# A recurrence's division by logarithm, exponential and one Newton step on a Trainium2 core

## The chip, the core and the metric

The kernel runs on one core of a Trainium2 chip, in one launch. The metric is the device time of that core in microseconds (us). Before the change it was 1567.87 us, the median of three runs (1567.68 to 1570.94).

A core has five engines, each with its own queue of instructions: TensorE (PE in the profile, with PEld for its weight loads), VectorE (DVE), ScalarE (ACT), GpSimd (POOL) and SyncE (SP). [...] ScalarE evaluates functions such as exponential, sigmoid or square root from a table, and the profile shows an instruction ACT_TABLE_LOAD where the table is changed.

## The reference

A block of three kinds of layers, on x of 4 sequences of 1024 tokens with 256 channels, all in float32:

```python
x = x + attn_a(layernorm(x))     # time mixing with a recurrence (changed)
x = x + ffn(layernorm(x))        # mixture of 64 experts, 4 per token, and 2 shared
x = x + attn_b(layernorm(x))     # retention with 16 heads
x = x + ffn(layernorm(x))
```

The changed part is the recurrence of attn_a. For each channel, w is -exp(time_decay) and u is time_first; p, q and o are carried from token to token:

```python
no = maximum(o, u + kt)
A, Bc = exp(o - no), exp(u + kt - no)
y = (A * p + Bc * vt) / (A * q + Bc)
no2 = maximum(w + o, kt)
A2, B2 = exp(w + o - no2), exp(kt - no2)
p, q, o = A2 * p + B2 * vt, A2 * q + B2, no2
...
out = (sigmoid(r) * y) @ W_out.T     # r, v, k are projections of the normed x
```

## The kernel before

The 4096 tokens are cut into 8 segments of 512 tokens, two to a sequence. The residual x stays on the chip in 8 tiles. The program has four stages, and the change lies in the first:

1. attn_a, and of the first ffn the choice of experts, the sending of the token rows to pages in memory, and the shared experts (`stage_1`).
2. The first ffn's routed experts: pages are loaded with their expert's weights, computed, and gathered back.
3. attn_b (`stage_2`), interleaved with the end of stage 2 and the beginning of the second ffn.
4. The second ffn's routed experts and the stores.

In stage 1 every segment passes five steps that `wkv(i)` returns. `norm` (layernorm at L188 and transposes at L212) gives the normed rows with channels on the partitions. `inputs(hf)`, for each of two halves hf of 128 channels, projects k, v and r into three banks (TensorE, L641) and moves them out on ScalarE: k and v as copies (L652, L653), r as a sigmoid (L654). `weights(hf)` finds o for all 512 tokens by one scan along the tokens (L673), subtracts (L677), and makes a2, b2 and c by a Relu and an Exp each on ScalarE (L679 to L688). `sums(hf)` scans q and p (L697, L701), forms the denominator den = c + q (L706), its reciprocal (L707), the numerator c v + p (L708, L709), the product with r (L710) and y (L711), all on VectorE with tiles of 128 partitions by 512 elements. `output(h)` projects y (TensorE, L719) and adds it to x (L724). The tile den is b2's, the tile num is a2's; tags such as a2 and b2 have two buffers each.

In exact terms c is exp(min(u + k - o, CAP)): the Relu of L683 and the bias `cap` of L688 hold the exponent below CAP, which is 60.

After `output`, `Ffn.route(i)` chooses experts for the segment: norm, logits, pick, rank, place, weigh (mostly VectorE, L266 to L396; the softmax's Exp on ScalarE is at L392), then 16 indirect sends on GpSimd (L402). `Ffn.shared(i)` computes the shared experts: TensorE L426 and L439, Silu on ScalarE at L431, VectorE L432 and L444.

The order of the work has two sources. The list `tracks` at the end of `stage_1` gives each step a time in half segments, and `merge` calls the steps in the order of these times, so that the recurrence of later segments is written between the routing and the shared experts of earlier ones; the shared experts of the last segments are put off (`behind`). From that order the framework's scheduler makes each engine's queue, and it may let an instruction that is ready sooner go ahead. Semaphores and table loads are put in by the compiler, not by the code.

The routed stage loads pages that hold rows of all segments (`sent`), so its first load of rows (`rx`, L489) waits for the last segment's sends; the transposes at L501 wait for that load.

Of the kernel before, what the change touches and what calls it, by code (L numbers as in the profile page):

```python
# [14 lines left out]
AF = mybir.ActivationFunctionType  # L15
ALU = mybir.AluOpType
# [8 lines left out]
SEG = 512  # L25
# [8 lines left out]
GR = 32  # L34
NG = P // GR
CH = 128
CAP = 60.0
QS = 256


# [20 lines left out]
def hybrid_kernel(ctx: ExitStack, tc: tile.TileContext, a: dict, out: bass.AP):  # L61
    nc = tc.nc
# [21 lines left out]
    def bank(tag, name, shape=None):  # L84

        return psum.tile(shape or [P, SEG], F32, tag=tag, bufs=dict(A=4, B=3, C=1)[tag], name=name)
# [15 lines left out]
        out=upper, in_=ones, compare_op=ALU.is_ge, fill=0.0, base=-1,  # L102
# [85 lines left out]
    def layernorm(pool, tiles, i, rows=None):  # L188

        n = len(tiles)  # L190
        mv = pool.tile([P, n, 2], F32, tag="ln_mv", name=f"mv_{i}")
        for t, xt in enumerate(tiles):
            st = pool.tile([P, 6], F32, tag="ln_st", name=f"st_{i}_{t}")
            nc.vector.bn_stats(out=st, in_=xt)
            nc.vector.bn_aggr(out=mv[:, t, :], in_=st)
        rstd = pool.tile([P, n], F32, tag="ln_rstd", name=f"rstd_{i}")
        nc.scalar.activation(out=rstd, in_=mv[:, :, 1], func=AF.Sqrt, bias=eps_t)
        nc.vector.reciprocal(out=rstd, in_=rstd)
        off = pool.tile([P, n], F32, tag="ln_off", name=f"off_{i}")
        nc.vector.scalar_tensor_tensor(  # L200
            out=off, in0=mv[:, :, 0], scalar=-1.0, in1=rstd, op0=ALU.mult, op1=ALU.mult
        )
        where, bufs = rows or (pool, 2)
        xn = where.tile([P, n, D], F32, tag="ln_xn", bufs=bufs, name=f"xn_{i}")
        for t, xt in enumerate(tiles):
            nc.scalar.activation(
                out=xn[:, t, :], in_=xt, func=AF.Identity, scale=rstd[:, t : t + 1],
                bias=off[:, t : t + 1],
            )
        return xn  # L210

    def transposed(xn, n, xnT, i):  # L212

        for k in range(KC):
            tp = bank("B", f"tp_{i}_{k}", [P, n * P])
            for t in range(n):
                nc.tensor.transpose(
                    tp[:, t * P : (t + 1) * P], xn[:, t, k * P : (k + 1) * P], ident
                )
            nc.any.tensor_copy(out=xnT[:, k, :], in_=tp)  # L220
# [371 lines left out]
    def stage_1(ctx: ExitStack, ffn, pf):  # L592
# [21 lines left out]
        if MOST < NPAIR:  # L614
# [5 lines left out]
        nc.vector.tensor_scalar(  # L620
            out=u_cap, in0=u_t, scalar1=-1.0, scalar2=CAP, op0=ALU.mult, op1=ALU.add
        )
        nc.vector.memset(cap, CAP)

        carry = {}

        def wkv(i):


            st = {}  # L630

            def norm():
                xn = layernorm(pf, [xs[i][:, t, :] for t in range(TT)], f"a{i}")
                st["xnT"] = pa.tile([P, KC, SEG], F32, tag="xnTa", bufs=2, name=f"xnT_a{i}")
                transposed(xn, TT, st["xnT"], f"a{i}")

            def project(hf, what):
                ps = bank("A", f"rvk_{i}_{hf}_{what}")
                lo = what * D + hf * P
                for k in range(KC):  # L640
                    nc.tensor.matmul(  # L641
                        ps, lhsT=rvk[:, k, lo : lo + P], rhs=st["xnT"][:, k, :],
                        start=(k == 0), stop=(k == KC - 1),
                    )
                return ps

            def work(tag, hf, width=SEG, bufs=2):
                return pa.tile([P, width], F32, tag=tag, bufs=bufs, name=f"{tag}_{i}_{hf}")

            def inputs(hf):  # L650
                r, v, k = work("r", hf, bufs=3), work("v", hf, bufs=3), work("k", hf)
                nc.scalar.copy(out=k, in_=project(hf, 2))  # L652
                nc.scalar.copy(out=v, in_=project(hf, 1))  # L653
                nc.scalar.activation(out=r, in_=project(hf, 0), func=AF.Sigmoid)  # L654
                st[hf] = dict(r=r, v=v, k=k)

            def start(t, hf, n, first):
                if i % SPB == 0:
                    nc.vector.memset(t[:, 0:1], first)
                else:  # L660
                    nc.vector.tensor_copy(out=t[:, 0:1], in_=carry[hf][n][:, SEG:])
                carry.setdefault(hf, {})[n] = t

            def weights(hf):

                s = st[hf]
                k = s["k"]  # L670
                o = work("o", hf, SEG + 1, bufs=3)
                start(o, hf, "o", -1e38)
                nc.vector.tensor_tensor_scan(  # L673
                    out=o[:, 1:], data0=w_t[:, hf : hf + 1].to_broadcast([P, SEG]), data1=k,
                    initial=o[:, 0:1], op0=ALU.add, op1=ALU.max,
                )
                nc.vector.tensor_sub(out=k, in0=k, in1=o[:, :SEG])  # L677
                a2, b2, c = (work(n, hf) for n in ("a2", "b2", "c"))
                nc.scalar.activation(out=a2, in_=k, func=AF.Relu, bias=w_neg[:, hf : hf + 1])  # L679
                nc.scalar.activation(  # L680
                    out=b2, in_=k, func=AF.Relu, scale=-1.0, bias=w_t[:, hf : hf + 1]
                )
                nc.scalar.activation(  # L683
                    out=c, in_=k, func=AF.Relu, scale=-1.0, bias=u_cap[:, hf : hf + 1]
                )
                nc.scalar.activation(out=a2, in_=a2, func=AF.Exp, scale=-1.0)
                nc.scalar.activation(out=b2, in_=b2, func=AF.Exp, scale=-1.0)
                nc.scalar.activation(out=c, in_=c, func=AF.Exp, scale=-1.0, bias=cap)  # L688
                s.update(a2=a2, b2=b2, c=c)

            def sums(hf):
                s = st[hf]
                v, a2, b2, c = (s[n] for n in ("v", "a2", "b2", "c"))
                p, q = (work(n, hf, SEG + 1, bufs=3) for n in "pq")
                start(q, hf, "q", 0.0)
                start(p, hf, "p", 0.0)
                nc.vector.tensor_tensor_scan(  # L697
                    out=q[:, 1:], data0=a2, data1=b2, initial=q[:, 0:1], op0=ALU.mult, op1=ALU.add
                )
                nc.vector.tensor_mul(out=b2, in0=b2, in1=v)  # L700
                nc.vector.tensor_tensor_scan(  # L701
                    out=p[:, 1:], data0=a2, data1=b2, initial=p[:, 0:1], op0=ALU.mult, op1=ALU.add
                )
                y = pa.tile([P, SEG], F32, tag=f"y{hf}", bufs=2, name=f"y_{i}_{hf}")
                num, den = a2, b2
                nc.vector.tensor_add(out=den, in0=c, in1=q[:, :SEG])  # L706
                nc.vector.reciprocal(out=den, in_=den)  # L707
                nc.vector.tensor_mul(out=num, in0=c, in1=v)  # L708
                nc.vector.tensor_add(out=num, in0=num, in1=p[:, :SEG])  # L709
                nc.vector.tensor_mul(out=num, in0=num, in1=s["r"])  # L710
                nc.vector.tensor_mul(out=y, in0=num, in1=den)  # L711
                st[f"y{hf}"] = y

            def output(h):
                op = bank("B", f"op_{i}_{h}", [P, 2, D])
                for t in range(2):
                    c0 = (2 * h + t) * P
                    for hf in range(KC):
                        nc.tensor.matmul(  # L719
                            op[:, t, :], lhsT=st[f"y{hf}"][:, c0 : c0 + P], rhs=wout[:, hf, :],  # L720
                            start=(hf == 0), stop=(hf == KC - 1),
                        )
                xt = xs[i][:, 2 * h : 2 * h + 2, :]
                nc.vector.tensor_add(out=xt, in0=op, in1=xt)  # L724

            return norm, inputs, weights, sums, output


# [7 lines left out]
        while n < CH:  # L736
            nc.vector.tensor_scalar_mul(
                out=pw16[:, Z + n + 1 : Z + 2 * n + 1], in0=pw16[:, Z + 1 : Z + n + 1],
# [350 lines left out]
    with ExitStack() as held:  # L1089
# [19 lines left out]
        with right("turned") as pt:  # L1109
# [7 lines left out]
            for i in range(NSEG - SPB):  # L1117
                b, s = divmod(i, SPB)
# [98 lines left out]
```

## Time and profile before

| what | us |
|---|---|
| median of three runs | 1567.87 |
| the profiled execution | 1570.8 |
| its span (first to last instruction) | 1569.1 |
| PE busy | 1301.6 (83%) |
| DVE busy | 1019.6 (65%) |
| ACT busy | 706.5 (45%) |
| POOL busy | 515.2 (33%) |
| the last send of stage 1 starts | 418.61 |
| first TensorE work of the routed stage | 423.77 |

The profile is one execution. A row of a group gives the line of the code, the engine, the operation, output and input tiles with their shapes, the count, then the busy time and the mean duration of one in nanoseconds, then how long the engine was idle just before and what ended the idleness. A row in order of time gives start, duration, engine, line, operation and, in brackets, the idle time before it. Operations on one engine overlap a little, so the distance from one start to the next is less than the mean duration. Tiles' names leave out their buffer numbers: a2 and num are `a`, b2 and den are `b`.

The shares over the whole span are means over stages with different limits. Stage 1 takes the first 424 us, some 27% of the span.

### The profile page before, as it was taken

To read this page: it belongs to the slowest core of one execution; us is meant where nothing else is said; L and a number is where in the kernel's file an instruction comes from. 1 tells how busy PE (TensorE), PEld (TensorE's weight loads), DVE (VectorE), ACT (ScalarE), POOL (GpSimd) and SP (SyncE) were. 2 spreads that over 40 slices of the span, in tenths; PEclk is the share of its full clock that TensorE was granted. 3 is DMA by queue.
4 is the path that set the end of the run, shared out by engine and by line. 5 is a ranking of instruction groups with operands and counts; after the bars stand their busy time and mean duration, and the time that the engine had idled before them with its cause. 6 is when DMAs were issued, how large, how long until landed. Compare 5 with 4: busy or idle time off the path is not lost. (4 is left out here: it accounts for less than half of the span.)

```text
span 1569.1 us, 24370 instructions
## 1 busy us (share of the span) xinstructions
PE 1301.6 (83%) x8264; PEld 921.8 (59%) x8264; DVE 1019.6 (65%) x2447; ACT 706.5 (45%) x1364; POOL 515.2 (33%) x528
## 2 busy tenths in 40 slices
PE   4598999979588879999989699989996399999810
PEld 2254555646476756777765475667654388877710
DVE  5989899998355546666756693557647155566643
ACT  6586777743134453457433343344252144444410
POOL 0005244346300051323236543032034300155576
PEclk8699999999799999999979799999999699999955
DMA  9976921113499994666322211011012599999944
GB/s 354 394 226 116 289 71 47 41 47 114 161 302 329 330 324 129 201 197 201 117 90 81 81 55 54 0 55 38 18 54 82 177 330 322 319 352 366 357 139 127
DMA packets 192953, 278.13 MB, mean 177 GB/s; under 512 B 53683, under 2 KB 119094, under 8 KB 192822
## 3 DMA queue, kind: packets, MB, share of 16 engines
q1 hardware_dynamic: 144630, 166.34, 33.3%
q0 software_dynamic: 24576, 67.14, 13.2%
q10 hardware_dynamic: 23616, 43.00, 7.2%
q8 instruction: 70, 1.15, 0.3%
q14 instruction: 61, 0.50, 0.1%
HBM read 164.74 MB, written 124.26 MB: 184 GB/s over the span
## 5 line engine op out<-in xcount | busy, mean ns | idle before, releaser
L402 POOL DMA_INDIRECT sent<-xn_f,to_f x256 | 267.5, 1045 | 512.8 <-ACT w_f L392 285.7
L562 POOL DMA_INDIRECT gy_f<-made,to_f x256 | 245.0, 957 | 532.3 <-DMA rw_f<-wx 139.6
L513 PE MATMUL rg_f<-rxT_f,rw_f 128*128 128x128 f32 x1312 | 187.2, 286 | 15.1 <-DVE rxT_f L505 7.0
L513 PEld LDWEIGHTS rg_f<-rxT_f,rw_f 128*128 128x128 f32 x1312 | 166.2, 198 | 25.9 <-DVE rxT_f L505 17.1
L505 DVE COPY rxT_f<-rt_f 128x512 f32<-128x512 f32 x164 | 113.0, 689 | 102.1 <-PE rt_f L501 100.8
L573 DVE SCALAR_TENSOR_TENSOR x<-gy_f,w_f,x 128x256 f32<-128x256 f32 x256 | 121.5, 482 | 63.0 <-DMA gy_f<-made,to_f 59.4
L501 PE MATMUL rt_f<-ident,rx_f 128*128 128x128 f32 x656 | 108.3, 290 | 62.1 <-DMA rx_f<-sent 55.3
L532 PE MATMUL rp_f<-rw_f,rh_f 64*128 64x128 f32 x1312 | 135.7, 304 | 11.1 <-DVE rh_f L521 9.6
L518 ACT ACTIVATE rs_f<-rg_f 64x256 f32<-64x256 f32 x164 | 61.7, 376 | 174.1 <-PE rg_f L513 144.4
L426 PE MATMUL g_f<-xnT_f,f_swg 128*128 128x512 f32 x256 | 126.7, 610 | 2.1 <-DVE pm L983 1.5
L439 PE MATMUL o_f<-f_swd,sh_f 128*128 128x256 f32 x512 | 122.6, 387 | 5.5 <-DVE sh_f L432 3.1
L501 PEld LDWEIGHTS rt_f<-ident,rx_f 128*128 128x128 f32 x656 | 75.3, 146 | 86.0 <-DMA rx_f<-sent 49.8
L426 PE MATMUL u_f<-xnT_f,f_swu 128*128 128x512 f32 x256 | 123.3, 599 | 2.1 <-ACT k L652 1.5
L532 PEld LDWEIGHTS rp_f<-rw_f,rh_f 64*128 64x128 f32 x1312 | 101.8, 192 | 37.9 <-issue 12.2
L538 ACT COPY ry_f<-rp_f 128x256 f32<-128x256 f32 x248 | 87.6, 374 | 79.6 <-PE rp_f L532 47.0
L521 DVE TENSOR_TENSOR rh_f<-rg_f,rs_f 64x256 f32<-64x256 f32 x164 | 69.8, 426 | 71.1 <-ACT rs_f L518 68.3
L439 PEld LDWEIGHTS o_f<-f_swd,sh_f 128*128 128x128 f32 x512 | 95.7, 192 | 27.0 <-DVE sh_f L432 5.1
L983 DVE TENSOR_TENSOR pm<-sc,decay 128x512 f32<-128x512 f32 x128 | 84.0, 684 | 21.4 <-PE sc L975 13.8
L641 PE MATMUL rvk<-xnT_a,rvk 128*128 128x512 f32 x192 | 92.2, 621 | 1.0 <-DVE xnT_a L220 0.6
L431 ACT ACTIVATE sh_f<-g_f 128x512 f32<-128x512 f32 x64 | 38.0, 597 | 112.3 <-PE g_f L426 87.5
L522 ACT COPY rh_f<-rh_f 64x256 f32<-64x256 f32 x164 | 66.1, 403 | 38.8 <-DVE rh_f L521 34.5
L426 PEld LDWEIGHTS u_f<-xnT_f,f_swu 128*128 128x128 f32 x256 | 47.8, 191 | 57.5 <-issue 52.1
(227 smaller groups left out, 2252.6 us busy)
## 6 DMA issues: line engine op xcount, KB each, us to landing
rw_f<-wx SPq DMA_DIRECT2D x328, 192.0 KB, 4.4
rx_f<-sent SPq DMA_DIRECT2D x164, 256.0 KB, 4.9
made<-ry_f ACTq DMA_DIRECT2D x164, 256.0 KB, 4.6
sent<-zeros SPq DMA_DIRECT2D x7, 2048.0 KB, 15.6
sent<-zeros SPq DMA_DIRECT2D x1, 10240.0 KB
x<-in_x_dram SPq DMA_DIRECT2D x8, 512.0 KB
wx<-in_wg_dram SPq DMA_DIRECT2D x2, 2048.0 KB, 40.4
sent<-xn_f,to_f POOLq DMA_INDIRECT x256, 2.5
```

The lines of the kernel that those rows point to most:

```text
L402: ins = nc.gpsimd.indirect_dma_start(out=rows_sent[: pairs_until(i) * 2 * P, :], out_offset=bass.IndirectOffsetOnAxis(ap=st["to"][:, c : c ...
L426: nc.tensor.matmul(ps, lhsT=w[:, k, s], rhs=self.xnT[i][:, k, :], start=(k == 0), stop=(k == KC - 1),)
L439: nc.tensor.matmul(o[:, t, :], lhsT=st["h"][:, c, s], rhs=self.weights[2][:, c, :], start=(c == 0), stop=(c == NS - 1),)
L501: nc.tensor.transpose(tp[:, k, j, :], s["x"][:, j, k * P : (k + 1) * P], ident)
L505: nc.vector.tensor_copy(out=xT, in_=tp)
L513: nc.tensor.matmul(gu[:, j, :], lhsT=s["w"][:, j, k * 2 * F : (k + 1) * 2 * F], rhs=s["xT"][:, k, j, :], start=(k == 0), stop=(k == KC - 1),)
L532: nc.tensor.matmul(yp[:, j, :], lhsT=s["h"][r, j, :], rhs=s["w"][r, j, WD:], start=True, stop=True,)
L538: copy(out=y[:, :, c * P : (c + 1) * P], in_=yp)
L562: nc.gpsimd.indirect_dma_start(out=y[:, k, :], out_offset=None, in_=rows_made[: ready[t] * 2 * P, :], in_offset=bass.IndirectOffsetOnAxis( ...
L573: tc.keep_in_program_order(nc.vector.scalar_tensor_tensor(out=xs[i][:, t, :], in0=got[t][:, k, :], scalar=s["w"][:, c : c + 1], in1=xs[i][ ...
L641: nc.tensor.matmul(ps, lhsT=rvk[:, k, lo : lo + P], rhs=st["xnT"][:, k, :], start=(k == 0), stop=(k == KC - 1),)
L983: nc.vector.tensor_mul(out=pm, in0=ch[j]["sc"][g], in1=decay.rearrange("p (k g b) n -> p g k b n", k=KC, b=2)[:, g],)
```

## The change

The reciprocal of den is no longer one VectorE instruction. ScalarE computes exp(-ln(den)) into a new tile inv, in two instructions, and VectorE refines it by one Newton step: inv (den inv - 2) is the negative of the improved reciprocal, and the last product is multiplied by -0.5. The sigmoid is replaced by tanh: sigmoid(r) = 0.5 (1 + tanh(r / 2)), of which tanh(r / 2) is computed where the sigmoid was, the "1 +" is part of the product with the numerator, and the 0.5 is in the last product. den is formed right after the scan of q, ahead of the product and scan for p, and has a tile of its own. CAP goes from 60 to 40.

```diff
-CAP = 60.0
+CAP = 40.0
...
-                nc.scalar.activation(out=r, in_=project(hf, 0), func=AF.Sigmoid)
+                nc.scalar.activation(out=r, in_=project(hf, 0), func=AF.Tanh, scale=0.5)
...
+                den, inv = work("den", hf), work("inv", hf)
+                nc.vector.tensor_add(out=den, in0=c, in1=q[:, :SEG])
+                nc.scalar.activation(out=inv, in_=den, func=AF.Ln)
+                nc.scalar.activation(out=inv, in_=inv, func=AF.Exp, scale=-1.0)
                 nc.vector.tensor_mul(out=b2, in0=b2, in1=v)
                 nc.vector.tensor_tensor_scan(
                     out=p[:, 1:], data0=a2, data1=b2, initial=p[:, 0:1], op0=ALU.mult, op1=ALU.add
                 )
                 y = pa.tile([P, SEG], F32, tag=f"y{hf}", bufs=2, name=f"y_{i}_{hf}")
-                num, den = a2, b2
-                nc.vector.tensor_add(out=den, in0=c, in1=q[:, :SEG])
-                nc.vector.reciprocal(out=den, in_=den)
+                num = a2
                 nc.vector.tensor_mul(out=num, in0=c, in1=v)
                 nc.vector.tensor_add(out=num, in0=num, in1=p[:, :SEG])
-                nc.vector.tensor_mul(out=num, in0=num, in1=s["r"])
-                nc.vector.tensor_mul(out=y, in0=num, in1=den)
+                nc.vector.scalar_tensor_tensor(
+                    out=num, in0=s["r"], scalar=1.0, in1=num, op0=ALU.add, op1=ALU.mult
+                )
+                nc.vector.tensor_mul(out=den, in0=den, in1=inv)
+                nc.vector.scalar_tensor_tensor(
+                    out=inv, in0=den, scalar=2.0, in1=inv, op0=ALU.subtract, op1=ALU.mult
+                )
+                nc.vector.scalar_tensor_tensor(
+                    out=y, in0=num, scalar=-0.5, in1=inv, op0=ALU.mult, op1=ALU.mult
+                )
```

## The prediction

> **What bounds the kernel now.** I read the page's forty slices first, to find where the changed lines run (the first ten slices, some 400 us), then the busy time of each engine by stage, then the groups of that stage, then the engines' instructions in order of time. The chain of work that ended last can't be used here: it reaches back to 793 us only.
>
> Busy tenths by slice, from the page; a slice is 39 us:
>
> ```profile
> PE   4598999979588879999989699989996399999810
> DVE  5989899998355546666756693557647155566643
> ACT  6586777743134453457433343344252144444410
> ```
>
> In slices 2 to 10 the digits of DVE are 8 or 9 almost throughout, later only 3 to 7. So VectorE matters in this stage and not elsewhere. The first stage cut into stretches (start and end, length, then busy us of each engine with its instructions, granted TensorE clock, DMA share, GB/s):
>
> ```profile
> 0.00:80.00 80.00, 40.51 (x97) 19.98 (x98) 59.25 (x120) 47.04 (x71) 1.48 (x11) 0.79 1.00 374
> 80.00:220.70 140.70, 130.00 (x531) 77.54 (x529) 123.20 (x313) 102.61 (x147) 44.44 (x40) 0.98 0.71 183
> 220.70:264.26 43.56, 40.54 (x166) 23.74 (x165) 42.74 (x102) 33.30 (x48) 17.68 (x16) 1.00 0.13 47
> 264.26:320.00 55.74, 51.98 (x209) 30.34 (x208) 53.13 (x114) 45.32 (x64) 27.34 (x25) 1.00 0.16 59
> 320.00:378.90 58.90, 50.60 (x232) 32.04 (x232) 57.75 (x148) 22.29 (x35) 28.72 (x30) 0.97 0.25 76
> ```
>
> The third row is one segment, from the q scan of its first half to that of the next segment. DVE is busy 42.74 of 43.56 us (98%), PE 40.54 (93%, at full clock), ACT 33.30 (76%). VectorE ends last, but TensorE is only 2.2 us behind it. In the last row DVE works 57.75 of 58.90 us while PE has 8 us free.
>
> How the stage hands over, from the order of time: the last segment's VectorE chain ends in the row numbers, GpSimd sends from 397.86 to 419.6, and TensorE waits for those sends:
>
> ```profile
> 423.77 1.97 PE L501 MATMUL rt_f<-ident,rx_f 128*128 128x128 f32 x8 [16.64 <-DMA rx_f<-sent]
> ```
>
> All page loads of the routed stage wait for the last send, so time gained on the last segment's chain arrives at the end of the kernel nearly whole.
>
> **The change part by part.** The groups concerned, of 0 to 440 us (count, then busy us and mean ns of one, then idle time before):
>
> ```profile
> L707 DVE RECIPROCAL b<-b 128x512 f32<-128x512 f32 x16 | 53.5, 3345 | 0.0
> L654 ACT ACT_TABLE_LOAD x16 | 20.5, 1283 | 0.3
> L710 DVE TENSOR_TENSOR a<-a,r 128x512 f32<-128x512 f32 x16 | 10.8, 677 | 0.0
> L711 DVE TENSOR_TENSOR y<-a,b 128x512 f32<-128x512 f32 x16 | 10.8, 673 | 0.0
> L686 ACT ACTIVATE a<-a 128x512 f32<-128x512 f32 x16 | 10.0, 628 | 0.2
> L330 DVE SCALAR_TENSOR_TENSOR far_f<-rk_f,jump_f 128x256 f32<-128x256 f32 x8 | 3.3, 412 | 0.1
> L334 DVE TENSOR_TENSOR far_f<-far_f,end_f 128x256 f32<-128x256 f32 x7 | 2.9, 420 | 0.0
> ```
>
> *VectorE.* Sixteen reciprocals go (8 segments, 2 halves). Two multiplications become three-operand forms in place, and two operations are new: den times inv, and the Newton form. The rows L330 and L334 show that the three-operand form costs what the plain one does at equal shape (412 against 420 ns), so L710 and L711 keep their 0.68 us. The other end: L573's three-operand rows of that shape take 482 ns, with a scalar from a tile; 15% more on three instructions would be 0.3 us a half, 5 us in all. I take the equal price, as all scalars here are constants like L330's. Operations overlap in issue: a reciprocal starts at 353.33 and its successor at 356.59, a plain multiplication holds its place for 0.60 us (30.22 to 30.82). Net a half: -3.26 + 2 x 0.60 = -2.06 us; times 16 = -33 us of VectorE. A segment's 42.74 becomes 38.6.
>
> *ScalarE, the operations.* Logarithm and exponential on 128x512, priced by L686: 0.63 us, or 0.52 when back to back (a start at 117.06 us, the next at 117.58): about 1.2 a half, 19 us in all. Tanh takes Sigmoid's place at one price (597 ns row).
>
> *ScalarE, the table loads.* Here the price is least certain. L654 has a load before each of 16 Sigmoids; every change between Exp, Sqrt, Silu and Sigmoid shows one. [...] But in this trace each load stands at the activation that needs it, with no sign that a later one was looked at; a set chosen for the logarithm alone costs a second load at the exponential. So 1 to 2 loads a pair; I take 2: 32. Net 18 loads.
>
> What is a load worth? From ScalarE's order of time:
>
> ```profile
> 102.31 0.59 ACT L653 COPY v<-rvk 128x512 f32<-128x512 f32 x1 [0.62 <-PE rvk L641]
> 102.91 1.28 ACT L654 ACT_TABLE_LOAD   x1
> 104.21 0.60 ACT L654 ACTIVATE r<-rvk 128x512 f32<-128x512 f32 x1
> ```
>
> The copy ends at 102.90, the load runs from 102.91, Sigmoid from 104.21: 1.30 us in all. [...] By the row it is 18 x 1.3 + 19 = 42 us, 5.3 a segment: ScalarE at 38.6. [...] From both sides: 19 us (one load a pair, all of Sigmoid's gone) to 61 us (two a pair, none gone), ScalarE at 35.7 to 40.9.
>
> *The new wait.* On VectorE, den times inv waits for the exponential: 1.3 + 0.6 + 1.3 + 0.6 = 3.8 us from den with both loads. Between them stand the b2 product, the p scan, c times v, the addition of p and the product with r, some 3.6 us, so an idle ScalarE just meets it. If it is busy, everything queued behind on VectorE waits: the other half's scans, the layernorm statistics (and with them TensorE's transposes), the routing; the output product (L719) waits for y. The last half's chain still gets shorter: from q's end it was 8.1 us (0.6 + 1.2 + 3 x 0.6 + 3.27 + 2 x 0.6), now 0.6 + 3.8 + 3 x 0.6 = 6.2.
>
> *At nothing:* the cap is a constant in instructions that exist; den and inv are tiles of their own, so the b2 tile comes free earlier and nothing waits more. No DMA and no queue instruction moves.
>
> *The sum by stretch.* A segment now has PE 40.5, DVE 38.6, ACT 38.6 instead of 40.5, 42.7, 33.3. The binding engine is packed to 98% now; TensorE at 98% would give 41.3, a gain of 2.2. With three engines within 2 us of each other I don't expect that packing: ScalarE was busy 18.9 of 20 us between 220 and 240 us, just where the pair goes, and idle later. I take 0.5 us a segment, over 5.5 segments (80 to 320 us): 3 us. Between 0 and 80 us four reciprocals end, 8.2 us freed. PE waits there for xn_a, whose statistics follow the reciprocals of 30.82 and 58.17 in VectorE's order; ScalarE, four fifths busy from 20 to 60 us, gives part back: 3 us. From 320 to 379 us two reciprocals (335.87 and 353.33) sit on a VectorE without idle time, and ScalarE is only 38% busy: of 4.1 us freed I count 3.5. Sum: -9.5 us. Against the profiled execution (span 1569.1, with 1.7 us around it 1570.8 us) that is 1561.3; it lay 2.9 us above the median of the runs, 1567.87, so the forecast is 1558.
>
> **The rivals.** *TensorE bounds cleanly*: the pair always finds ScalarE free, the period falls to 41.3: 5.5 x 2.2 = 12, with 6 at the start and 4 at the end -22: 1546. For it: VectorE's waits on ScalarE are few today (11.9 us before q in the whole stage). Against: three close engines. *No difference*: PE's 40.5 plus its waits for xn_a already make 43.5, and only 0 to 3 us arrive: 1566. Against it: PE idles 8 us where VectorE has none. *Slower, ScalarE becomes the bound*: place, the half of each segment in which ScalarE runs exponentials, Silu and Sigmoid without a gap; price, up to 7.6 us a segment if Tanh saves no load and each pair takes two; it decides once ScalarE's busy time and its waits pass 43.5 us, from 40.9 busy on if it packs worse than 94%. ScalarE's order then holds up k, xn_a and Silu for TensorE, and VectorE waits at den times inv. At 45 us a segment: 5.5 x 1.5 = 8, the start and end gains gone: 1576. For it: its idle time now is mostly one wait of 8 us for the projection, which may not be usable. *It doesn't do what it says*: Tanh loads as Sigmoid did; that is contained in the bound above.
>
> **How the numbers follow.** A measurement can tell about 0.2% here, 3.1 us. Likeliest (1551 to 1564): 0.37; TensorE bound (1541 to 1551): 0.22; no difference (1565 to 1571): 0.14; slower (1571 to 1590): 0.27. So faster 0.59, same 0.14, slower 0.27. The range, 1543 to 1579, leaves out the far ends of the second and the last case; the likeliest case's own is 1551 to 1564.
>
> **What would show it.** No reciprocal of 128x512; two more VectorE rows of 0.68 us; VectorE's first 400 us 33 us lighter. Loads at Tanh nearly gone, loads at the logarithm and behind it 16 each; if the second set is missing, ScalarE is 20 us lighter than I say. The segment's period, 43.56 now, should be near 43; below 42 speaks for TensorE, above 44 for ScalarE, and then VectorE's waits name the exponential of inv. GpSimd's last send should start near 388 instead of 397.86. The later stages should keep their lengths; if they don't, the forecast is wrong for a reason that I have not seen.

## The result, and the profile after

| | before | after |
|---|---|---|
| median of six runs each | 1568.9 (1567.6 to 1576.58) | 1554.87 (1548.35 to 1561.01) |
| the profiled execution, its span | 1570.8, 1569.1 | 1561.01, 1558.9 |
| first TensorE work of the routed stage (the handover) | 423.77 | 411.87 |
| from there to the end | 1145.3 | 1147.0 |
| DVE busy | 1019.6 | 995.3 |
| ACT busy | 706.5 | 739.3 |

The kernel is faster: ratio 0.9917, 95% interval 0.9893 to 0.9941, some 13 us. The profile of after is the slowest of its six runs, 6 us above their median.

The busy tenths of the 40 slices, from the page of after:

```profile
PE   6399999899588879999989699999996499998810
DVE  5789888898255446666665793556747155566643
ACT  6688888863144444556443343344152144444410
```

In the first ten slices ACT now stands mostly at 8 where it stood at 7, and DVE more often at 8 than at 9. The same stretches as before, in the same columns (start and end, length, then busy us of PE, PEld, DVE, ACT and POOL with their instructions, granted clock, DMA share, GB/s):

```profile
0.00:80.00 80.00, 40.06 (x96) 20.00 (x96) 53.08 (x129) 51.47 (x78) 1.48 (x11) 0.79 1.00 372
80.00:220.70 140.70, 130.23 (x541) 78.95 (x540) 124.53 (x330) 120.21 (x170) 49.20 (x48) 0.99 0.73 192
220.70:264.26 43.56, 40.21 (x154) 23.78 (x153) 38.48 (x98) 36.86 (x52) 16.03 (x15) 0.96 0.13 46
264.26:320.00 55.74, 51.65 (x243) 32.70 (x242) 48.27 (x123) 47.48 (x68) 16.83 (x18) 1.00 0.12 43
320.00:378.90 58.90, 56.49 (x264) 36.60 (x263) 54.41 (x163) 29.12 (x43) 37.00 (x37) 1.00 0.30 92
```

VectorE is no longer without idle time: 38.48 of 43.56 us in the third row where it had 42.74. The stretches are fixed in time, so with an earlier schedule they hold other work: in the last row TensorE has 56.49 us instead of 50.60, because VectorE no longer keeps it waiting there. In before TensorE waited 5.18 us for the normed rows, which came behind the reciprocal of 335.87 us on VectorE; in after no wait of TensorE in that stretch is as long as 2 us:

```profile
340.74 2.17 PE L217 MATMUL tp_f<-ident,xn_f 128*128 128x128 f32 x8 [5.18 <-ACT xn_f L206]
```

The groups that took the reciprocal's place (0 to 440 us; count, then busy us and mean ns of one, then the idle time before them):

```profile
L704 ACT ACT_TABLE_LOAD x16 | 20.5, 1283 | 0.3
L705 ACT ACT_TABLE_LOAD x16 | 20.5, 1283 | 0.3
L655 ACT ACT_TABLE_LOAD x7 | 9.0, 1283 | 0.1
L717 DVE TENSOR_TENSOR den<-den,inv 128x512 f32<-128x512 f32 x16 | 10.8, 676 | 4.7 <-ACT inv L705 4.7
L718 DVE SCALAR_TENSOR_TENSOR inv<-den,inv 128x512 f32<-128x512 f32 x16 | 10.8, 674 | 0.1
L721 DVE SCALAR_TENSOR_TENSOR y<-a,inv 128x512 f32<-128x512 f32 x16 | 10.9, 678 | 0.1
```

A load at the logarithm (L704) and another at the exponential behind it (L705), 16 times each, and 7 left at the tanh (L655). The two Newton operations cost 0.68 us each; the new wait of VectorE for `inv` is 4.7 us in the whole stage. The handover:

```profile
411.87 1.98 PE L501 MATMUL rt_f<-ident,rx_f 128*128 128x128 f32 x8 [13.06 <-DMA rx_f<-sent]
```

It comes 11.9 us earlier than before, and that is nearly the whole effect.

Where the 11.9 us come from is seen by the softmax's Exp of each segment (start of L392's ACTIVATE, us), which stands once in every segment's chain:

| segment | 1 | 2 | 3 | 4 | 5 | 6 | 7 | 8 |
|---|---|---|---|---|---|---|---|---|
| before | 112.87 | 155.99 | 208.92 | 255.38 | 299.36 | 339.35 | 368.90 | 397.23 |
| after | 109.08 | 155.97 | 200.11 | 243.34 | 291.59 | 331.27 | 358.65 | 385.47 |
| difference | -3.8 | 0.0 | -8.8 | -12.0 | -7.8 | -8.1 | -10.3 | -11.8 |

### The profile page after: what moved, and what is told of

It is laid out like the page before. It is cut to its first block, busy times and chain, and to the rows that moved or that the text cites. A ratio compares the mean times of both kernels' runs of the same rounds, so it can differ in the third digit from the quotient of the medians.

```text
span 1558.9 us, 24439 instructions
## 1 busy us (share of the span) xinstructions
PE 1297.8 (83%) x8264; PEld 921.5 (59%) x8264; DVE 995.3 (64%) x2465; ACT 739.3 (47%) x1407; POOL 509.1 (33%) x528
## 5 line engine op out<-in xcount | busy, mean ns | idle before, releaser
L402 POOL DMA_INDIRECT sent<-xn_f,to_f x256 | 259.3, 1013 | 508.4 <-ACT w_f L392 246.8
L532 PE MATMUL rp_f<-rw_f,rh_f 64*128 64x128 f32 x1312 | 136.5, 302 | 10.8 <-DVE rh_f L521 8.9
L532 PEld LDWEIGHTS rp_f<-rw_f,rh_f 64*128 64x128 f32 x1312 | 102.6, 190 | 37.8 <-issue 10.8
```

What stands on the lines that cost most here:

```text
L402: ins = nc.gpsimd.indirect_dma_start(out=rows_sent[: pairs_until(i) * 2 * P, :], out_offset=bass.IndirectOffsetOnAxis(ap=st["to"][:, c : c ...
L532: nc.tensor.matmul(yp[:, j, :], lhsT=s["h"][r, j, :], rhs=s["w"][r, j, WD:], start=True, stop=True,)
```

## The experiments

My theory: VectorE's work in stage 1 is what counts, it passes to the last send, and so to the end. Rivals: the gain comes from fewer table loads (tanh); or from den being formed earlier; or from nothing but a new order of the queues, since every edit gives the scheduler another order. In the experiments, "VectorE's work" is counted by the rows: 53.5 us for the 16 reciprocals of before, 10.8 us for each set of 16 short operations.

### Four kernels on one chip

*tanh_only*: before, with only the sigmoid exchanged.

```diff
-nc.scalar.activation(out=r, in_=project(hf, 0), func=AF.Sigmoid)
+nc.scalar.activation(out=r, in_=project(hf, 0), func=AF.Tanh, scale=0.5)
...
-nc.vector.tensor_mul(out=num, in0=num, in1=s["r"])
-nc.vector.tensor_mul(out=y, in0=num, in1=den)
+nc.vector.scalar_tensor_tensor(
+    out=num, in0=s["r"], scalar=1.0, in1=num, op0=ALU.add, op1=ALU.mult)
+nc.vector.scalar_tensor_tensor(
+    out=y, in0=num, scalar=0.5, in1=den, op0=ALU.mult, op1=ALU.mult)
```

> The kernel before with tanh in place of sigmoid alone: the reciprocal stays on VectorE, the cap stays 60, the one and the half go into three-operand forms. VectorE's work is unchanged; ScalarE has 26 table loads fewer in the first stage (54 instead of 80), 34 us. Theory (VectorE's load sets the first stage): 1564 to 1568, little or no gain. Rival (the table loads saved by tanh are the gain): 1556 or less.

*sigmoid_kept*: after, with the sigmoid back, and plain products.

```diff
-nc.scalar.activation(out=r, in_=project(hf, 0), func=AF.Tanh, scale=0.5)
+nc.scalar.activation(out=r, in_=project(hf, 0), func=AF.Sigmoid)
...
-nc.vector.scalar_tensor_tensor(
-    out=num, in0=s["r"], scalar=1.0, in1=num, op0=ALU.add, op1=ALU.mult)
+nc.vector.tensor_mul(out=num, in0=num, in1=s["r"])
...
-    out=y, in0=num, scalar=-0.5, in1=inv, op0=ALU.mult, op1=ALU.mult
+    out=y, in0=num, scalar=-1.0, in1=inv, op0=ALU.mult, op1=ALU.mult
```

> The changed kernel with the sigmoid kept: 16 table loads more in the first stage (109 instead of 93), 21 us of ScalarE, VectorE as in the changed kernel. Theory: most of the gain stays, 1555 to 1562, the loss being ScalarE coming near the bound. Rival (tanh is the gain): back at 1568 or above.

*no_newton*: after, with exp(-ln(den)) used as it is.

```diff
-nc.vector.tensor_mul(out=den, in0=den, in1=inv)
-nc.vector.scalar_tensor_tensor(
-    out=inv, in0=den, scalar=2.0, in1=inv, op0=ALU.subtract, op1=ALU.mult)
...
-    out=y, in0=num, scalar=-0.5, in1=inv, op0=ALU.mult, op1=ALU.mult
+    out=y, in0=num, scalar=0.5, in1=inv, op0=ALU.mult, op1=ALU.mult
```

> The changed kernel without the Newton step: it leaves out the refinement of the reciprocal (two VectorE operations a half, 32 in all, 19 us by their issue distance of 0.60 us). Theory (VectorE still sets part of the time, at some 0.36 us a us freed, 12 of 33): 1546 to 1551. Rival (TensorE and ScalarE bound the first stage now): 1553 to 1556, no further gain.

*two_newton*: after, with the Newton step made twice, in a tile `nr` of its own (two more operations a half).

```diff
-nc.vector.tensor_mul(out=den, in0=den, in1=inv)
-nc.vector.scalar_tensor_tensor(
-    out=inv, in0=den, scalar=2.0, in1=inv, op0=ALU.subtract, op1=ALU.mult)
+nr = work("nr", hf)
+nc.vector.tensor_mul(out=nr, in0=den, in1=inv)
+nc.vector.scalar_tensor_tensor(
+    out=inv, in0=nr, scalar=2.0, in1=inv, op0=ALU.subtract, op1=ALU.mult)
+nc.vector.tensor_mul(out=nr, in0=den, in1=inv)
+nc.vector.scalar_tensor_tensor(
+    out=inv, in0=nr, scalar=2.0, in1=inv, op0=ALU.add, op1=ALU.mult)
```

> The changed kernel with a second Newton step: 32 more VectorE operations, 19 us. Theory: it gives back about 0.36 us a us, 1560 to 1565. Rival (TensorE and ScalarE bound now): 1555 to 1557.

Measured, on a chip where before took 1567.24 us (after's and before's own rows are those of the result):

| kernel | VectorE's work by rows | loads in stage 1 | handover | from there to the end | median | ratio to before |
|---|---|---|---|---|---|---|
| before | 0 | 80 | 423.77 | 1145.3 | | |
| after | -31.9 | 93 | 411.87 | 1147.0 | | 0.9917 [0.9893, 0.9941] |
| no_newton | -53.5 | 93 | 402.94 | 1137.0 | 1544.83 | 0.9865 [0.9848, 0.9883] |
| two_newton | -10.3 | 93 | 423.90 | 1139.0 | 1563.3 | 0.9972 [0.9959, 0.9986] |
| sigmoid_kept | -31.9 | 109 | 417.85 | 1135.5 | 1560.08 | 0.9952 [0.9939, 0.9965] |
| tanh_only | 0 | 54 | 439.88 | 1138.0 | 1579.0 | 1.0088 [1.0063, 1.0114] |

The code of no_newton, after and two_newton differs in VectorE operations alone, and all three have 93 loads: each dose of 21.6 us moves the handover, by 8.9 us and then by 12.0, about half, and the intervals of the three ratios don't meet. That is what the theory asks for. The same line also shows a price, if it is drawn on: two_newton meets before's handover with some 10 us freed, so the exchange itself (the pair, its loads, its new order) would cost about 5 us, and only what VectorE frees beyond that would be gain.

The rival of the order is not excluded by this. Every edit gave other queues: of VectorE's 830 rows before the handover, the Newton operations left out, 716 stand in the same sequence in after and no_newton, 649 in after and two_newton. TensorE's clock differs too: by the clock records of the traces it is at half for 6.8 us between 80 and 390 us in after, for none in no_newton and for 17.1 in two_newton. And tanh_only moved the handover by 16 us without any change of VectorE's work, which is more than either step. No edit of the order alone was run on this chip. So that VectorE's work counts is well supported; that it is worth one half is a reading of three profiles.

Of the expectations, those of sigmoid_kept and two_newton came true by the theory's numbers; no_newton fell 1.2 us below the theory's range, and tanh_only above both of its ranges.

The ratios follow the handover within 5 us. What lies behind the handover is 1135 to 1147 us long in these single profiles, though the order of the work there is the same: between after and no_newton the last 7061 of TensorE's 8264 matmuls stand in the same sequence, and the lengths differ by 10 us. So a profile's span alone would not have told these kernels apart; the medians and the handover do.

With TensorE's clock whole, no_newton shows what the stage looks like when VectorE is lightest. Two segments of it:

```profile
196.48:239.53 43.05, 40.66 (x169) 24.51 (x169) 37.47 (x103) 37.97 (x53) 16.44 (x16) 1.00 0.14 49
239.53:282.36 42.83, 40.66 (x169) 24.51 (x169) 37.28 (x98) 37.97 (x53) 16.17 (x16) 1.00 0.14 50
```

TensorE is busy 40.66 of 42.83 us (95%), VectorE 37.28, ScalarE 37.97: TensorE is next, and packs to 95%, not to the 98% that VectorE had.

sigmoid_kept: 16 more loads (20.5 us of ScalarE) move the handover by 6.0 us and the median by 5.2, though the two intervals just touch (0.9939 against 0.9941). ScalarE's time is thus not free, about 0.3 us for each us of loads, as far as these two kernels, whose order differs too, can tell. The loads of the pair do not undo the change: with all sigmoid loads back it is still faster than before.

tanh_only is the surprise, and goes against every theory that counts work: VectorE's work is that of before, ScalarE has 26 loads (33 us) less, and it is 0.9% slower. Its profile shows where. One segment of it:

```profile
214.61:264.05 49.44, 44.16 (x170) 26.98 (x169) 44.64 (x105) 29.97 (x48) 17.36 (x17) 0.90 0.12 43
```

The same 169 or 170 matmuls take TensorE 44.16 us at a mean granted clock of 0.90, not 40.66 at 1.00. In order of time, in that segment:

```profile
230.15 2.16 PE L217 MATMUL tp_f<-ident,xn_f 128*128 128x128 f32 x8 [2.29 <-ACT xn_f L206]
234.62 3.67 PE L255 MATMUL lp_f<-wr_sb,xnT_f 128*128 128x64 f32 x16 [2.31 <-DVE xnT_f L220]
238.09 3.07 PE L426 MATMUL g_f<-xnT_f,f_swg 128*128 128x512 f32 x4
```

TensorE waits 2.29 us for the normed rows, works 2.16 us, and waits 2.31 us more for the transposed ones. Its clock, in stretches of 2 us:

```profile
228.00:230.00 2.00, 0.00 (x0) 0.00 (x0) 2.00 (x4) 1.17 (x4) 1.70 (x2) 1.00 0.37 131
230.00:232.00 2.00, 1.85 (x8) 1.16 (x8) 2.00 (x4) 1.57 (x4) 1.70 (x2) 0.53 0.18 66
232.00:234.00 2.00, 0.31 (x2) 0.00 (x0) 2.00 (x9) 1.54 (x3) 1.39 (x3) 0.50 0.27 96
234.00:236.00 2.00, 1.38 (x7) 1.38 (x7) 1.13 (x7) 0.88 (x2) 1.50 (x2) 0.50 0.28 100
236.00:238.00 2.00, 2.00 (x11) 2.00 (x11) 0.00 (x0) 0.00 (x0) 0.96 (x1) 0.50 0.36 131
238.00:240.00 2.00, 2.00 (x5) 0.97 (x5) 1.23 (x9) 1.67 (x4) 0.00 (x0) 0.50 0.00 0
```

The clock is at half already when TensorE takes up work after the first gap: by the clock records of the trace from 230.13 to 240.37 us. The second gap lies inside that stretch. While TensorE is idle VectorE is busy (2.00 of 2.00 us in the first three rows): it does other work first, as its queue has another order than before's. VectorE then waits for the router's logits, 25.5 us in seven waits (5.0 us in before), since those come from the slowed TensorE.

Over the stage (20 to 400 us; before, then tanh_only) TensorE is busy nearly as long, at a lower clock, and gets fewer matmuls done:

```profile
20.00:400.00 380.00, 324.33 (x1304) 191.68 (x1303) 345.21 (x802) 249.00 (x357) 128.12 (x118) 0.94 0.52 161
20.00:400.00 380.00, 320.80 (x1228) 191.52 (x1227) 333.10 (x767) 209.68 (x325) 117.76 (x113) 0.90 0.51 158
```

By the clock records, half clock between 80 and 390 us lasts 10.2 us in before and 44.4 in tanh_only. An estimate from these two: 34 us more at half clock take up to 17 us from TensorE, and the handover comes 16.1 us later. So the loss shows as a new order that opens gaps, and a clock that falls with them. What of the edit makes the scheduler choose that order (fewer loads, other operations) is not told by this.

### Eight kernels on two other chips

To part the order of the queues from the work, I put the sums of each half one tenth of a half segment later in the list of due times, which leaves all arithmetic as it is:

```diff
-for n, f in ((0, inputs), (10, weights), (20, sums))
+for n, f in ((0, inputs), (10, weights), (21, sums))
```

*before_shift* and *after_shift* are before and after with that edit.

> The kernel before with nothing added or taken away: only the due time of the step sums is 0.1 half segments later, so that the scheduler makes other queues of the same instructions (with 86 table loads instead of 80). Theory (the change's gain is VectorE's work): within 5 us of 1567. Rival (the change's 13 us are an accident of the order of the queues): 10 us or more away, to either side.

> The changed kernel with the same shift of sums by 0.1 half segments (95 table loads instead of 93). Theory: within 5 us of 1555. Rival (accident of order): 10 us or more away; if this and the shifted kernel before meet, the gain was the order's.

*early_recip*: before, with den and its VectorE reciprocal right behind the scan of q, in a tile of its own.

```diff
+den = work("den", hf)
+nc.vector.tensor_add(out=den, in0=c, in1=q[:, :SEG])
+nc.vector.reciprocal(out=den, in_=den)
 nc.vector.tensor_mul(out=b2, in0=b2, in1=v)
...
-num, den = a2, b2
-nc.vector.tensor_add(out=den, in0=c, in1=q[:, :SEG])
-nc.vector.reciprocal(out=den, in_=den)
+num = a2
```

> The kernel before with den and its reciprocal, still on VectorE, moved to the place where the change forms den, right after the scan of q, and den in a tile of its own. VectorE's work is that of before. Theory: 1562 to 1574, no gain beyond what an order brings. Rival (the early denominator and the freed tile are the gain): 1553 to 1558.

*relu_for_ln*: after, with Relu in the logarithm's place: at L704 relu_again has no load where after_again has 16, and at L705 it has 6 instead of 16. It leaves the logarithm out, so the values are others, and tokens go to other experts.

```diff
-nc.scalar.activation(out=inv, in_=den, func=AF.Ln)
+nc.scalar.activation(out=inv, in_=den, func=AF.Relu)
```

> The changed kernel with Relu in place of the logarithm, so that the denominators and all that follows are wrong and tokens choose other experts: it leaves out the logarithm, and with it 30 table loads of the first stage (63 instead of 93), 39 us of ScalarE at 1.3 us each; VectorE's work is that of the changed kernel. Theory (VectorE and TensorE bound the stage, ScalarE has room): 1549 to 1557. Rival (the loads of the pair hold the gain back): 1536 to 1545.

Then, on a third chip, after once more, with two of these kernels again, and tanh_only with the sigmoid's table loaded by hand ahead of each tanh (both held in program order), which brings its loads to before's 80:

```diff
+nc.scalar.preload_act_table_set("sigmoid_and_others")
 nc.scalar.activation(out=r, in_=project(hf, 0), func=AF.Tanh, scale=0.5)
```

> The changed kernel once more, beside the three others, because the second group of runs fell on a chip on which every kernel, that of before too, took some 11% longer. 0.989 to 0.994 of the time before, as at first.

> The changed kernel with Relu in place of the logarithm again (it leaves the logarithm out, the results are wrong and other experts are chosen), 30 table loads fewer. Theory (ScalarE has room, the loads are mostly hidden): within 5 us of the changed kernel beside it. Rival (the loads hold the gain back): 10 us or more below it.

> The kernel before with sums due 0.1 half segments later, again. It was 1.7% slower on the other chip. If the order of the queues alone is worth 10 us and more, 1.006 to 1.02 of the time before; if that was the chip's, 0.997 to 1.003.

> Tanh alone, as in the run with tanh only, but with sigmoid's table loaded ahead of it by hand, so that the first stage has 80 table loads as before instead of 54, and the scheduler's order is closer to that of before. If the loss of tanh alone came from the order (TensorE's gaps in each segment and the half clock after them, 49 us a segment): 1562 to 1571, and a granted clock near 1.00 from 220 to 320 us. If it came from tanh's arithmetic: 1575 to 1582 again.

| kernel | before on that chip | median | ratio to before |
|---|---|---|---|
| before_shift | 1742.71 | 1769.0 | 1.017 [1.0098, 1.0242] |
| after_shift | 1742.71 | 1728.04 | 0.9949 [0.9918, 0.9979] |
| early_recip | 1742.71 | 1746.21 | 1.0032 [1.0002, 1.0063] |
| relu_for_ln | 1742.71 | 1723.69 | 0.9927 [0.9897, 0.9957] |
| after_again | 1754.12 | 1762.77 | 1.001 [0.9968, 1.0051] |
| relu_again | 1754.12 | 1741.43 | 0.9927 [0.9897, 0.9956] |
| before_shift_again | 1754.12 | 1786.07 | 1.0154 [1.0079, 1.023] |
| tanh_sigmoid_table | 1754.12 | 1767.99 | 1.0113 [1.0048, 1.0177] |

On these chips before takes 11 and 12% longer than on the first, after 13% longer on the one where it ran, and after's gain is not to be seen there (1.001). The profiles show why these chips can't judge the change as the first did. In before_shift_again, three stretches of 4 us:

```profile
224.00:228.00 4.00, 3.61 (x9) 1.33 (x7) 3.28 (x8) 0.30 (x1) 3.02 (x4) 1.00 0.27 98
228.00:232.00 4.00, 0.00 (x0) 0.00 (x0) 0.00 (x0) 0.00 (x0) 1.86 (x2) 1.00 0.28 98
232.00:236.00 4.00, 0.24 (x1) 0.18 (x1) 3.26 (x7) 1.48 (x3) 0.00 (x0) 0.52 0.00 0
```

TensorE, VectorE and ScalarE do nothing in the second row. VectorE and ScalarE start again at rows that take a result from TensorE:

```profile
232.74 0.69 DVE L444 TENSOR_TENSOR x<-o_f,x 128x512 f32<-128x512 f32 x1 [5.28 <-remote]
232.80 0.59 ACT L652 COPY k<-rvk 128x512 f32<-128x512 f32 x1 [5.58 <-remote]
```

"remote" means that the trace has no record for what released them. The last matmul on record, of `rvk`, ends at 227.61. In the same stretch of time of before, after and no_newton no wait of VectorE or ScalarE is put down to this releaser. ScalarE's waits of that kind in stage 1 (20 to 480 us; line, releaser, us in total, times, longest), in before_shift_again:

```profile
ACT k L652 <- remote: 16.7, 3, 5.6
ACT lg_f L260 <- remote: 11.4, 2, 8.0
ACT xnT_f L220 <- remote: 6.4, 1, 6.4
```

In relu_again they are 9.3 us in two waits at L652 and 5.4 us in one at L220. So the stops are no even stretching of the time: one program meets them where another does not. In before_shift_again the three at L652 end at 232.80, 287.06 and 341.48 us, one a segment, and are 5.58, 5.59 and 5.58 us long; in before_shift, on the other chip, there are three at the same line, at 223.16, 278.26 and 333.10, of 5.53, 5.54 and 6.21 us. The profiled execution of after_again, 8 us above its median, has three there too, 32.1 us together. Three stops of this length are together more than the 12 us that the change is worth. On such a chip a ratio tells which program is better there, not which edit of work made it so; no profile of before was taken on them, so how much of before_shift's 1.7% or of after's lost gain is due to stops, and how much to order or clock, stays open. Against what was expected of them: after_again missed its gain. before_shift, an edit of the order alone, was slower by 26 and 32 us, and so fell to the rival of the order both times. after_shift, early_recip and the first relu_for_ln lie, as ratios, where the theory had them, but relu_again was 21 us below after_again, where its rival had it. tanh_sigmoid_table was no nearer to before than tanh_only; its granted clock from 220 to 270 and from 270 to 320 us was 0.97 and 0.93, between before's 1.00 and tanh_only's 0.90, so the new order was not undone.

The eight ratios therefore carry only this: early_recip (1.0032) gives no hint that forming den early is the gain; tanh with before's number of loads is still slower (1.0113), which speaks against the missing loads themselves as the cause of tanh_only's loss but, on such a chip, doesn't show it; the variants of after with 30 fewer loads were faster than before on both chips, but whether through the loads or through fewer stops is not settled. An edit of the order alone can move the time on these chips by more than the change is worth; how much it can on the first is not known.

## Why the prediction was right, point by point

The forecast was 1558 us, with 1551 to 1564 as the likeliest case; the median is 1554.87.

**VectorE bounds the stage, TensorE is 2 us behind.** Right, as far as the doses go: with VectorE's work alone changed in the code, the handover moves by about half of it, and no_newton's rows show TensorE next, at 95%. What share of the 11.9 us the new order has is open.

**VectorE 33 us lighter.** The rows give what was said: 53.5 us out, 10.8 and 10.8 in, and the three-operand forms at 0.68 us, so the lower end of that cost was the right one. The busy time fell by 24.3 us only. 1.4 us of the rest are two more copies of transposed rows (L220: 17 instead of 15) that VectorE took. The durations of all VectorE rows, added up, fell by 29.6 us; the page counts time once in which two rows overlap, and the overlaps shrank by 5.3 us. So an operation that comes in is worth nearer 0.68 than 0.60 us of busy time. Why the rows overlap less is not shown; my guess is the idle moments before them: VectorE's waits for the logits (13.9 us, 5.0 before) and for the shared experts' product (12.5 us, 6.4 before).

**ScalarE, +42 us.** It measured +32.8. The pair takes two loads each time, 32, as taken by the absence of any look-ahead in the trace: in 11 of the 16 pairs nothing but a Relu (L680, three times) or a copy (L260, once) stands between the two functions on ScalarE, neither line has a load in after, and the exponential has its own load all the same. The price of a load, 1.28 us in the row and 1.30 on the path, held again: 1.28, and 1.31 at each of the 16 exponentials of the pair. What I had wrong is the count of the others. The net 18 of the sum takes 14 of Sigmoid's 16 loads as gone, a term that no run shows; after shows 9 gone. Seven tanh loads stay, not two, each where the last load before it is a Sqrt's (L197); of the nine tanh without a load, seven come after a load at L705 (the pair's Exp), one after that at L617 (the Exp of `w_neg`) and one after another tanh's. The exponentials of `weights` fell from 19 loads to 5: in 11 of the 16 halves none stands at them, the last load before them being at L392 (the softmax's Exp) five times, at L705 four times, at L617 once and at a tanh once. Silu has four more. Net 13 loads, not 18:

| loads in stage 1 at | before | after |
|---|---|---|
| sigmoid or tanh | 16 | 7 |
| exponentials of weights | 19 | 5 |
| Ln, and its Exp | 0 | 32 |
| Silu | 21 | 25 |
| Sqrt, softmax and the rest | 24 | 24 |

**The new wait, 3.8 us against 3.6 us of cover.** Right, and smaller than it might have been: 4.7 us in 4 waits of 16. An example of the pair, from ScalarE's order of time in after:

```profile
202.00 1.28 ACT L704 ACT_TABLE_LOAD   x1
203.51 0.63 ACT L704 ACTIVATE inv<-den 128x512 f32<-128x512 f32 x1 [0.23 <-DVE den L703]
204.16 1.28 ACT L705 ACT_TABLE_LOAD   x1
205.45 0.63 ACT L705 ACTIVATE inv<-inv 128x512 f32<-128x512 f32 x1
```

The load of the logarithm's table did not wait for den here: it ran from 202.00 us, for 1.28 us, and ScalarE then waited 0.23 us more for den, so one of the two loads was out of the path.

**The sum by stretch: -3, -3, -3.5.** By the table of the softmax's Exp: -3.8 by the first segment, 4.0 more by the fifth, 4.0 more by the last. The handover is at -11.9, and the last segment's first send starts at 386.10 where before had 397.86 and I said 388 (the prediction's "last send" means this one). That each term is only a little larger than taken is partly luck. The difference is 0.0 at the second segment and -12.0 at the fourth, and falls to -7.8 at the fifth, so other markers would give other terms. And the path that I gave for the first term is not the one: TensorE's wait for xn_a ends in both kernels at the same time (before, then after):

```profile
69.56 2.16 PE L217 MATMUL tp_a<-ident,xn_a 128*128 128x128 f32 x8 [18.19 <-ACT xn_a L206]
69.55 2.16 PE L217 MATMUL tp_a<-ident,xn_a 128*128 128x128 f32 x8 [26.16 <-ACT xn_a L206]
```

The statistics for it start on VectorE at 65.24 us instead of 61.98, since other rows stand ahead of them in the new order. The 3.8 us arise after that, on a path that was not traced.

Between the fourth and the fifth segment's Exp, 48.25 us apart, TensorE idled up to 245.16 for `sh_f`, 2.98 us in all, and its clock was at half from 245.96 to 249.38 by the trace's records. The period "near 43" was met from the third segment to the fourth (43.2, and 44.1 from the second to the third) and by no_newton (43.05, 42.83), and missed in that one.

**The later stages keep their lengths.** 1147.0 against 1145.3 us, and by the table of experiments a scatter of 10 us that belongs to a single execution.

**The rivals.** That TensorE bounds cleanly fell: it packs to 95% in no_newton's segments, and only with VectorE lighter still. Slower through ScalarE did not happen, but sigmoid_kept shows its mechanism at work, 0.3 us for each us of loads: at that price ScalarE's 32.8 us more would cost some 10 us, where the line through the doses gives about 5 for the whole exchange. I had counted them as hidden but for what the packing loses. That an edit which takes work away can be slower through the order it brings, as tanh_only was, stood among no rival of mine; nor did a gain that comes from the order, which is not excluded on the first chip.

A version that beats both kernels came out of it: no_newton, at 0.9865, which leaves the refinement of the reciprocal out.

## What to carry to other kernels

When an engine is the bound by only 2 us a period, start from about a half as the price of its freed time, as the three doses here had it, and subtract what the receiving engine pays for table loads; then look for the second operation that can go, as the Newton step did for another 8 to 10 us. Follow one marker through all periods (here the softmax's Exp) and the handover to the next stage: they tell kernels apart where the span of one profile scatters by 10 us. An edit that changes only the order, or frees an engine that isn't the bound, can lose by opening gaps for TensorE, as tanh_only did (half clock for 44.4 us instead of 10.2, the handover 16.1 us later), so read the granted clock in short stretches before crediting or blaming the arithmetic.

## What the hardware showed that was not expected

In tanh_only TensorE's clock fell to 0.50 at the end of a single gap of 2.29 us. In sigmoid_kept gaps of 2.14 and 2.15 us (up to 215.47 and 261.38) were followed by half clock from 217.04 and from 261.42, while in after a gap of 3.20 us (107.97 to 111.17) was not followed by any. So in these traces the length of one gap doesn't decide alone. Each stretch of half clock between 80 and 390 us in the six kernels of the first chip is 3.41, 6.83 or 10.24 us long by the clock records.

On two of the three chips of the experiments TensorE's results stopped coming for 3 to 11 us at places that repeat with the program, and before took 11 and 12% longer. The DMA queues of the kind "instruction" (in after_again q8 with 70 packets and q14 with 62 over the span) don't explain it: in none of the eleven stops of ScalarE at L652 in before_shift, before_shift_again, after_again and relu_again is a packet of theirs under way. GpSimd is within a segment's sends (L402) in each of them, but so it is at times in the kernels without stops; the cause stays open.
